# Layer 1's normed rows turned by VectorE and through DRAM instead of by TensorE

## The chip, the cores and the metric

The kernel runs on one core of one Trainium2 chip. A core has a matrix engine (TensorE, PE in the profile; its weight loads are PEld), a vector engine (VectorE, DVE), a scalar engine (ScalarE, ACT), a general engine (GpSimd, POOL) and SyncE (SP), which here issues transfers. Sixteen DMA engines move data between DRAM and the on-chip SBUF. TensorE writes to PSUM, a small accumulator memory of banks. The metric is the device time of one launch in microseconds, smaller is better.

## The reference, cut to what matters

Two layers, each attention and then a feed-forward part, each part followed by a residual and a layer norm over rows of 512 numbers, on 8 batches of 512 tokens:

```
x = layernorm(x + attention0(x))           # 16 heads of 32, causal
x = layernorm(x + top-2 of 8 experts(x))   # with low-rank additions
x = layernorm(x + attention1(x))           # below
x = layernorm(x + quantised_ffn(x))        # integer weights, 1408 hidden

def attention1(x):                         # 8 query heads of 64, 2 key/value groups
    nrm = norm(x, over the row) * 512 ** -0.5
    h = norm_scale * x / (nrm + 1e-8) * split_scale
    q, k, v = h @ Wq.T, h @ Wk.T, h @ Wv.T
    attn = softmax(q k^T / 8)              # no mask
    return (attn v) @ Wo.T
```

The experts' result is normed, and those rows are normed again into h. The change is in how h reaches the form that q, k and v need it in: columns of 512 on partitions, tokens along the free dimension (hT). Because attention 1 has no mask, the order of the 512 tokens inside a batch does not matter to softmax as long as keys and values agree and the query rows are put back.

## The kernel before, in words

All arithmetic is float32; a float32 matmul shows as two instructions, so x8 in a timeline is four matmuls. The program runs attention 0 (up to about 760 us), then the experts over gathered tiles of 128 tokens (to about 1190 us), attention 1 (to about 1766 us) and the quantised feed-forward part.

*The expert tiles.* `Tiles.step` handles one tile of 128 tokens in about 5.8 us: gate and up products (`gate_up`), ScalarE's Silu and VectorE's product, two transposes with a ScalarE copy (`turn_hidden`), down products (`down`), an output copy by VectorE or ScalarE in turn, and a store of the tile's results by SP (L871; the y buffer has two copies). TensorE's order is as written; the other engines are placed by a scheduler. In `usual_pass`, a table called `beside` puts other pieces between tiles, among them `Attention1.first_pieces`: the preparation of batch 0 for attention 1, one piece every second tile.

*Preparing a batch for attention 1* (`Attention1.prepare`). `fetch` gathers the two experts' result rows of 128 tokens (indirect transfers issued by POOL into the buffers rows0 and rows1); `add` sums them into x with their weights and takes row statistics (VectorE); `deviations` takes roots (POOL); `norm` writes the normed rows xn over the buffer rows0 (VectorE, four 128x512 instructions, L714). `turn(c)`, for c = 0 to 3, transposes four 128x128 blocks of xn into one PSUM bank by TensorE (L1477), and ScalarE copies the bank into hT and multiplies by the per-column scale nss, the product of the two norm scales (L1478). `key` (L1484), `value` (L1493) and `query(g)` (L1503) multiply hT by the weights held in `attn1_qkv` and ScalarE copies the results out. hT has one buffer: the next batch's hT can be written once this batch's query(3) has read it.

*The attention loop* (`batches`). Each batch has 8 steps. A step issues two pairs of score matmuls (L1584), whose exponentials ScalarE takes (L1587); then VectorE adds the exponentials of the step before (`add`, L1595); then come the pieces that `plan` lists for this step; then the products with v of the step before (L1606). After every second step `normalise` multiplies the sums by a block of ones (row sums, L1614), ScalarE copies them (L931), VectorE takes a reciprocal (L1617) and multiplies the product by it into `aoT` (L1618), and POOL keeps a running total of the reciprocals (L934). Here TensorE, VectorE, ScalarE and POOL all run strictly in the order written; SP's order is left to the scheduler. PSUM for single products (`mm`) has two banks.

Within batch b's steps, `plan` places the remaining queries of b, the output projection of batch b - 1 for four groups of rows (`project`: matmuls L1552, then VectorE's residual L1558 and statistics L1566), and the preparation of batch b + 1: fetch at step 0, adds, deviations at 4, norm at the front of step 5, the four turns and key at 6, value and query(0) at 7. It also places conversions of the integer weights of the last part (`weights.convert`, VectorE L994 and L926), each followed by the next load into the same single buffer (`weights.load`, L980, issued by SP): that load waits until the conversion has read the buffer. Batch 0 has its own places, and so has the last batch.

Of the kernel before, what the change touches and what calls it, by code (L numbers as in the profile page):

```python
# [9 lines left out]
F32 = mybir.dt.float32  # L10
# [3 lines left out]
AF = mybir.ActivationFunctionType  # L14
ALU = mybir.AluOpType
# [3 lines left out]
P = 128  # L19
NB = 8  # L20
S = 512
D = 512
NT = S // P
ND = D // P
# [39 lines left out]
class Inputs:  # L64
# [3 lines left out]
    def __init__(self, *aps):  # L68
        for name, ap in zip(self.names, aps, strict=True):
            setattr(self, name, ap)  # L70


class Env:
# [928 lines left out]
class IntegerFfn:  # L1002
# [64 lines left out]
    def out(self, os, t, c, parts):  # L1067
        for i, h in enumerate(parts):
            self.nc.tensor.matmul(os[t], lhsT=h[:, ts(t, P)], rhs=self.weights(2 * NHID + c),  # L1069
                                  start=(c, i) == (0, 0), stop=(c, i) == (NHID - 1, 1))  # L1070
# [374 lines left out]
class Attention1:  # L1445
# [2 lines left out]

    HD = 64

    def __init__(self, env, guard, router, rows, own, p_mm):
        self.env, self.nc, self.guard, self.router, self.own, self.p_mm = env, env.nc, guard, router, own, p_mm
        self.rows = rows

        self.w_qkv = own.tile([P, UPS, 512], F32, name="attn1_qkv")
        env.load_units(self.w_qkv, 0, env.ins.w_attn1[:6])
        self.nss = env.norm_scales()
        self.state = {}
# [4 lines left out]
    def prepare(self, b):  # L1463


        nc, own, w_qkv = self.nc, self.own, self.w_qkv
        st = self.state[b] = {"qT": [None] * ND}
        combine = Combine(self.router, b, self.rows, ("rows0", "rows1"))

        def norm():  # L1470
            st["xn"], st["scale"] = combine.norm()
            st["hT"] = own.tile([P, ND, S], F32, tag="hT", name="hT1")

        def turn(c):
            ps = self.mm([P, S], "ps_hT")
            for t in range(NT):
                nc.tensor.transpose(ps[:, ts(t, P)], st["xn"][:, t, ts(c, P)], self.env.ident)  # L1477
            nc.scalar.activation(st["hT"][:, c, :], ps, AF.Copy, scale=self.nss[:, c : c + 1])  # L1478

        def key():  # L1480
            hT = st["hT"]
            ps = self.mm([P, S], "ps_k1")
            for c in range(ND):
                nc.tensor.matmul(ps, lhsT=w_qkv[:, 4, ts(c, P)], rhs=hT[:, c, :], start=c == 0, stop=c == ND - 1)  # L1484
            st["kT"] = own.tile([P, S], F32, tag="kT", name="kT", bufs=2)
            nc.scalar.copy(st["kT"], ps)

        def value():
            hT = st["hT"]
            ps = self.mm([P, NT, P], "ps_v1")  # L1490
            for t in range(NT):
                for c in range(ND):
                    nc.tensor.matmul(ps[:, t, :], lhsT=hT[:, c, ts(t, P)], rhs=w_qkv[:, 5, ts(c, P)],  # L1493
                                     start=c == 0, stop=c == ND - 1)
            st["v"] = own.tile([P, NT, P], F32, tag="v", name="v1", bufs=2)
            nc.scalar.copy(st["v"], ps)

        def query(g):

            hT = st["hT"]  # L1500
            ps = self.mm([P, S], "ps_q1")
            for c in range(ND):
                nc.tensor.matmul(ps, lhsT=w_qkv[:, c, ts(g, P)], rhs=hT[:, c, :], start=c == 0, stop=c == ND - 1)  # L1503
            st["qT"][g] = (self.work if g % 2 else own).tile([P, S], F32, tag="qT", name="qT")
            nc.scalar.copy(st["qT"][g], ps)  # L1505

        return {"fetch": combine.fetch, "add": combine.add, "sum": combine.sum, "stat": combine.stat, "deviations": combine.deviations, "norm": norm,
                "turn": turn, "key": key, "value": value, "query": query}

    def first_pieces(self):  # L1510

        do = self.first = self.prepare(0)
        return ([lambda t=t: do["fetch"](t) for t in range(NT)] + [lambda t=t: do["add"](t) for t in range(NT)]
                + [do["deviations"], do["norm"]] + [lambda c=c: do["turn"](c) for c in range(ND)]
                + [do["key"], do["value"], lambda: do["query"](0)])

    def run(self, weights, split):

# [7 lines left out]
    def batches(self, work, p_sc, p_av, weights, split):  # L1526
        env, nc, guard, state, HD = self.env, self.nc, self.guard, self.state, self.HD
        xs = env.xs
        scale = 1.0 / math.sqrt(HD)
# [81 lines left out]
        def normalise(b, g, total, av):  # L1611
            rs = self.mm([P, S], "rs1")
            for j in range(2):
                nc.tensor.matmul(rs[HD * j : HD * (j + 1), :], lhsT=ones, rhs=total[:, j, :], start=True, stop=True)  # L1614
            r_inv = work.tile([P, S], F32, tag="r_inv", name="r_inv1")
            guard.watch_sums(rs, r_inv)
            nc.vector.reciprocal(r_inv, r_inv)  # L1617
            nc.vector.tensor_tensor(state[b]["aoT"][:, g, :], av, r_inv, ALU.mult)  # L1618
            guard.watch_inverses(r_inv)

        def plan(b):


            todo = [[] for _ in range(ND * NT // 2)]
            here = pieces.pop(b)
            first, final = b == 0, b == NB - 1
            then = None if final else self.prepare(b + 1)
            if not final:
                pieces[b + 1] = then
                todo[0] += [lambda t=t: then["fetch"](t) for t in range(NT)]  # L1630
            for g, i in zip((1, 2, 3), (1, 3, 5) if first else (0, 1, 5) if final else (0, 1, 3)):
                todo[i].append(lambda g=g: here["query"](g))
            if b:
                for t, i in enumerate((2, 3, 4, 7) if final else (2, 3, 4, 5)):
                    todo[i].append(lambda t=t: project(b - 1, t))
                if not final:
                    todo[6].append(lambda: norm(b - 1))
            if final:
                for c, i in enumerate((0, 2, 4, 6)):
                    todo[i].append(lambda c=c: split(0, c, self.mm([P, S], "ps_xT")))  # L1640
            else:
                if first:

                    for t, i in ((2, 1), (3, 2)):
                        todo[i].append(lambda t=t: then["sum"](t))
                        todo[i + 2].append(lambda t=t: then["stat"](t))
                for t, i in ((0, 1), (1, 2)) if first else ((0, 2), (1, 2), (2, 3), (3, 4)):
                    todo[i].append(lambda t=t: then["add"](t))
                todo[4].append(then["deviations"])

                todo[5].insert(0, then["norm"])
                todo[6] += [lambda c=c: then["turn"](c) for c in range(ND)]
                todo[6].append(then["key"])
                todo[7] += [then["value"], lambda: then["query"](0)]
            for i in (7,) if first else (1, 7):
                todo[i] += [weights.convert, lambda: weights.load(work, 2, weights.FIRST)]
            return todo

# [34 lines left out]
def usual_pass(tc, ins, held_out):  # L1693
    nc = tc.nc
    with ExitStack() as ctx:
# [4 lines left out]
        with tc.tile_pool(name="a_mm", bufs=2, space=PSUM) as p_mm, ExitStack() as attn1_ctx:  # L1700
            with tc.tile_pool(name="routes", bufs=1, side="right") as routes, \
                    tc.tile_pool(name="experts", bufs=1, side="right") as pool, ExitStack() as tiles_ctx:
                experts = Experts(env, pool)
                router, tiles, tables = attention0(env, guard, keep, routes, experts, dram, p_mm, tiles_ctx)

                def load_rows(b):
                    rows = router.rows[S * b : S * (b + 1)]
                    nc.sync.dma_start(out=env.xs[b], in_=rows.rearrange("(t p) d -> p t d", p=P))

                env.open_stream(ctx, range(NB // 2))  # L1710
                rows = ctx.enter_context(tc.tile_pool(name="c_rows", bufs=1))
                own = attn1_ctx.enter_context(tc.tile_pool(name="c_own", bufs=1))
                attention = Attention1(env, guard, router, rows, own, p_mm)
                beside = {tiles.next + 6 * (b + 1): lambda b=b: load_rows(b) for b in range(NB // 2)}

                for i, piece in enumerate(attention.first_pieces()):
                    beside[E * NT + 4 + 2 * i] = piece
                with in_order(tc):
                    while tiles.next < tiles.n:
                        tiles.step()  # L1720
                        next(tables, None)
                        beside.pop(tiles.next, lambda: None)()
                assert not beside and next(tables, None) is None
                tiles.rare()
# [314 lines left out]
```

## Time and profile before

| what | us |
|---|---|
| median of three runs | 2284.05 |
| the runs | 2281.4 to 2284.93 |
| the profiled execution | 2286.21 |
| its span, first to last instruction | 2284.5 |
| TensorE busy (98% of the span) | 2238.4 |
| VectorE busy (54%) | 1242.0 |
| ScalarE busy (28%) | 648.2 |
| POOL busy (22%) | 496.2 |
| TensorE, transposes of xn into ps_hT, 128 | 20.2 |
| ScalarE, scaled copies into hT, 32 | 20.5 |
| VectorE, normed rows xn, 32 | 15.4 |

Busy times are sums over instructions; matmuls are pipelined, so a group's busy time is not the same as the time it holds TensorE. In a timeline each line has a start in us from the first instruction, a duration in us, the engine, the line of the kernel, the operation, written tile and read tiles, the shape and the count; what stands in brackets is how long the engine was idle before, and what it waited for. In a list of waits the numbers are us in total, times, and the longest. In a table of stretches the columns are the stretch, its length, busy time and count of PE, PEld, DVE, ACT and POOL, the granted clock of TensorE, the busy share of the DMA engines and GB/s.

### The profile page before, as it was taken

How to read it: one execution, taken by the hardware profiler on the slowest of the kernel's cores; microseconds unless marked ns; L12 is line 12 of the kernel's file. 1: busy time of each engine (PE TensorE's matmuls, PEld its weight loads, DVE VectorE, ACT ScalarE, POOL GpSimd, SP SyncE). 2: the span in 40 equal slices, each digit the busy share in tenths (PEclk: the TensorE clock that was granted, in tenths of full speed). 3: DMA queues.
4: the chain of work that ended last, by engine and by line, in shares of the span. 5: the costliest groups of instructions: out<-in, count | busy, mean ns of one | idle time of the engine just before them, and what ended most of it. 6: DMA issues, size and time to landing. Idle time of an engine off the chain costs nothing. (4 is left out here: it accounts for less than half of the span.)

```text
span 2284.5 us, 24183 instructions
## 1 busy us (share of the span) xinstructions
PE 2238.4 (98%) x9430; PEld 1153.0 (50%) x9430; DVE 1242.0 (54%) x1976; ACT 648.2 (28%) x937; POOL 496.2 (22%) x489
## 2 busy tenths in 40 slices
PE   9999999999998999999999999999999999999997
PEld 3344444444443444444443334443343777887776
DVE  3457576566657433242216877787667544444443
ACT  2332322323323221111223323333332222222222
POOL 2232423313233241131115122322211000000000
PEclk9999999999999999999999999999999999999999
DMA  8010101101112224232224011100100100000000
GB/s 290 19 56 1 56 19 37 56 1 56 47 45 74 93 85 174 91 125 88 92 84 147 10 56 56 49 27 27 37 1 17 48 19 19 19 19 19 19 19 20
DMA packets 58444, 126.63 MB, mean 55 GB/s; under 512 B 6210, under 2 KB 6210, under 8 KB 58322
## 3 DMA queue, kind: packets, MB, share of 16 engines
q1 hardware_dynamic: 47040, 89.32, 11.1%
q0 software_dynamic: 10560, 34.61, 5.2%
q8 instruction: 77, 1.26, 0.2%
q10 hardware_dynamic: 722, 1.07, 0.1%
q14 instruction: 45, 0.37, 0.0%
HBM read 89.59 MB, written 35.39 MB: 55 GB/s over the span
## 5 line engine op out<-in xcount | busy, mean ns | idle before, releaser
L845 PE MATMUL ps_gu<-experts,xrT 128*128 128x512 f32 (+1 forms) x520 | 248.7, 601 | 0.0
L1268 ACT ACTIVATE p<-sc 128x2048 f32<-128x2048 f32 (+1 forms) x96 | 152.9, 1593 | 189.0 <-PE sc L1264 189.0
L1273 POOL TENSOR_SCALAR_AFFINE_SELECT p<-p 128x512 f32<-128x512 f32 x128 | 93.2, 743 | 380.1 <-ACT p L1268 374.0
L1060 DVE SCALAR_TENSOR_TENSOR hT<-ps_u,vec,sg 128x512 f32<-128x512 f32 x88 | 65.8, 748 | 198.4 <-PE ps_u L1055 198.4
L1069 PE MATMUL ps_f<-ffn_w,h_half 128*128 128x512 f32 x672 | 169.8, 393 | 1.6 <-DVE h_half L1064 1.1
L934 POOL TENSOR_TENSOR g_total<-g_total,r_inv 128x512 f32<-128x512 f32 x64 | 89.7, 1402 | 359.7 <-DVE r_inv L1617 283.3
L1617 DVE RECIPROCAL r_inv<-r_inv 128x512 f32<-128x512 f32 x32 | 106.9, 3339 | 97.5 <-ACT r_inv L931 97.5
L1587 ACT ACTIVATE p<-sc 128x1024 f32<-128x1024 f32 x128 | 124.0, 1021 | 125.9 <-PE sc L1584 125.9
L1296 DVE TENSOR_TENSOR p<-p 128x1536 f32<-128x1536 f32 (+2 forms) x96 | 129.2, 1345 | 38.7 <-POOL p L1273 21.7
L1069 PEld LDWEIGHTS ps_f<-ffn_w,h_half 128*128 128x128 f32 x672 | 124.3, 188 | 34.9 <-DVE h_half L1064 7.6
L1055 PE MATMUL ps_g<-x_high,ffn_w 128*128 128x512 f32 x352 | 141.0, 401 | 0.8 <-DVE x L1558 0.8
L848 DVE TENSOR_TENSOR h<-ps_gu,h 128x256 f32<-128x256 f32 x67 | 28.4, 423 | 205.6 <-ACT h L847 205.6
L1055 PE MATMUL ps_g<-x_low,ffn_w 128*128 128x512 f32 x352 | 139.0, 395 | 0.0
L1055 PE MATMUL ps_u<-x_low,ffn_w 128*128 128x512 f32 x352 | 138.8, 394 | 0.0
L1055 PE MATMUL ps_u<-x_high,ffn_w 128*128 128x512 f32 x352 | 138.6, 394 | 0.0
L862 PE MATMUL ps_y<-experts,hT 128*128 128x512 f32 (+1 forms) x272 | 127.9, 593 | 0.5 <-ACT hT L856 0.5
L1584 PE MATMUL sc<-qT,kT 64*128 64x512 f32 x512 | 127.2, 615 | 1.0 <-ACT qT L1505 0.7
L1200 PE MATMUL ps_q<-experts 128*128 128x512 f32 x256 | 121.2, 615 | 4.3 <-DMA experts<-in_xT 4.3
L845 PEld LDWEIGHTS ps_gu<-experts,xrT 128*128 128x128 f32 x520 | 89.6, 192 | 68.2 <-issue 68.1
L1606 PE MATMUL av<-p,v 128*64 128x512 f32 x512 | 123.7, 605 | 0.0
L1193 PE MATMUL ps_v<-experts 128*128 128x512 f32 x256 | 116.3, 602 | 2.1 <-DVE v L1195 2.1
L1552 PE MATMUL ps_o<-attn_out,aoT 128*128 128x512 f32 x256 | 117.3, 602 | 0.8 <-ACT r_inv L931 0.8
(256 smaller groups left out, 3532.3 us busy)
## 6 DMA issues: line engine op xcount, KB each, us to landing
results<-y SPq DMA_DIRECT2D x68, 256.0 KB, 2.0
x<-in_x SPq DMA_DIRECT2D x8, 1024.0 KB, 7.5
experts<-in_gate_up SPq DMA_DIRECT2D x8, 1024.0 KB, 11.7
rows<-x SPq DMA_DIRECT2D x32, 256.0 KB, 2.1
x<-rows SPq DMA_DIRECT2D x8, 1024.0 KB, 11.3
experts<-in_xT SPq DMA_DIRECT2D x7, 1024.0 KB, 5.5
out<-x SPq DMA_DIRECT2D x28, 256.0 KB, 2.3
ffn_i<-in_wq_ffn SPq DMA_DIRECT2D x11, 512.0 KB, 4.3
```

What stands on the lines that cost most here:

```text
L845: mm = nc.tensor.matmul(ps, lhsT=xT[:, c, :], rhs=self.weights(i, c), start=c == 0, stop=c == ND - 1)
L862: self.nc.tensor.matmul(ps, lhsT=hT[:, c, :], rhs=self.weights(i, ND + c), start=c == 0, stop=c == self.NI - 1)
L1055: nc.tensor.matmul(ps, lhsT=w[:, ts(dc, P)], rhs=x[:, dc, :], start=(dc, i) == (0, 0), stop=(dc, i) == (ND - 1, 1))
L1069: self.nc.tensor.matmul(os[t], lhsT=h[:, ts(t, P)], rhs=self.weights(2 * NHID + c), start=(c, i) == (0, 0), stop=(c, i) == (NHID - 1, 1))
L1193: nc.tensor.matmul(ps, lhsT=xts[b][:, c, ts(t, P)], rhs=wv[:, c, :], start=c == 0, stop=c == ND - 1)
L1200: nc.tensor.matmul(ps, lhsT=wq[:, g, ts(c, P)], rhs=xts[b][:, c, :], start=c == 0, stop=c == ND - 1)
L1268: nc.scalar.activation(p, sc[:, :, :width], AF.Exp, scale=scale)
L1296: nc.vector.tensor_tensor(total[:, :, P * kt :], total[:, :, P * kt :], p[:, :, at : at + w], ALU.add)
L1552: nc.tensor.matmul(ps, lhsT=state[b]["aoT"][:, c, ts(t, P)], rhs=w_out[:, c, :], start=c == 0, stop=c == ND - 1)
L1584: nc.tensor.matmul(sc[:, j, :], lhsT=st["kT"][hs, ts(kt, P)], rhs=st["qT"][g][hs, :], start=True, stop=True)
L1587: nc.scalar.activation(p, sc, AF.Exp, scale=scale)
L1606: nc.tensor.matmul(st["av"][HD * j : HD * (j + 1), :], lhsT=st["v"][:, kt, HD * j : HD * (j + 1)], rhs=p[:, j, :], start=kt == 0, stop=kt ...
```

## The change

1. **The transposes.** `turn` is gone. A new class `Turn` holds a DRAM buffer. `blocks(t)` lets VectorE transpose each 32x32 block of one group of 128 normed rows, into a room of 128x2048 (the buffer rows1). After the fourth group, `out` stores the room in four transfers, one for each block of 32 partitions, so that in DRAM row p holds column p of each chunk; `back` loads 128 rows of 8 KB into hT. In the turned hT the tokens of a batch stand in another order: blocks of 32 from the four groups by turns.
2. **The order of tokens.** Queries, keys and values take that order from hT. In `normalise` the product with the reciprocal reads both operands in runs of 32 and writes `aoT` in the natural order.
3. **The scales.** nss is multiplied into the weights once, by ScalarE, in eight instructions beside the expert tiles (`scale`, with batch 0's fetches).
4. **The places.** For batches 2 to 7: adds at steps 1, 1, 2, 3 (before: 2, 2, 3, 4), deviations at 3, norm and the blocks at the front of step 4, key at 6. For batch 1, prepared in batch 0's loop: norm and blocks at 5, key at 7, and query(3) of batch 0 at step 4 instead of 5. One conversion moves from step 1 to step 0.

In the built program SP's queue holds, in batch 0's loop, the four stores of `out`, then one integer-weight load, then `back`; in the later loops `back` stands directly behind the four stores.

```
+class Turn:
+    N = P // 32
+    def __init__(self, env, dram, n, name):
+        self.nc, self.n = env.nc, n
+        self.dram = dram.tile([P, ND, self.N, n * 32], F32, name=name)
+    def blocks(self, room, t, x):
+        out = room.rearrange("p (j t c) -> p j t c", t=self.n, c=32)[:, :, t, :]
+        self.nc.vector.transpose(out, x.rearrange("p (j c) -> p j c", c=32))
+    def out(self, room):
+        for i in range(self.N):
+            src = room[32 * i : 32 * (i + 1), :].rearrange("r (k j f) -> r k j f", j=self.N, f=self.n * 32)
+            self.nc.sync.dma_start(out=self.dram.rearrange("(j r) k i f -> r k j i f", j=self.N)[:, :, :, i, :], in_=src)
+    def back(self, room):
+        self.nc.sync.dma_start(out=room, in_=self.dram.rearrange("p k i f -> p (k i f)"))
+    def by_tile(self, a, turned):
+        if turned:
+            return a.rearrange("p (i t c) -> p t i c", i=self.N, c=32)
+        return a.rearrange("p (t i c) -> p t i c", i=self.N, c=32)
...
         def norm():
             st["xn"], st["scale"] = combine.norm()
-            st["hT"] = own.tile([P, ND, S], F32, tag="hT", name="hT1")
-        def turn(c):
-            ps = self.mm([P, S], "ps_hT")
-            for t in range(NT):
-                nc.tensor.transpose(ps[:, ts(t, P)], st["xn"][:, t, ts(c, P)], self.env.ident)
-            nc.scalar.activation(st["hT"][:, c, :], ps, AF.Copy, scale=self.nss[:, c : c + 1])
+        def blocks(t):
+            if t == 0:
+                st["room"] = self.rows.tile([P, ND * S], F32, tag="rows1", name="turned")
+            self.turn.blocks(st["room"], t, st["xn"][:, t, :])
+            if t == NT - 1:
+                self.turn.out(st["room"])
+                st["hT"] = own.tile([P, ND, S], F32, tag="hT", name="hT1")
+                self.turn.back(st["hT"].rearrange("p k s -> p (k s)"))
...
+    def scale(self, c):
+        for part in (self.w_qkv[:, c, :], self.w_qkv[:, ND : ND + 2, ts(c, P)]):
+            self.nc.scalar.mul(part, part, self.nss[:, c : c + 1])
...
-            nc.vector.tensor_tensor(state[b]["aoT"][:, g, :], av, r_inv, ALU.mult)
+            nc.vector.tensor_tensor(self.turn.by_tile(state[b]["aoT"][:, g, :], False), self.turn.by_tile(av, True),
+                                    self.turn.by_tile(r_inv, True), ALU.mult)
...
-            for g, i in zip((1, 2, 3), (1, 3, 5) if first else (0, 1, 5) if final else (0, 1, 3)):
+            for g, i in zip((1, 2, 3), (1, 3, 4) if first else (0, 1, 5) if final else (0, 1, 3)):
...
-                for t, i in ((0, 1), (1, 2)) if first else ((0, 2), (1, 2), (2, 3), (3, 4)):
+                for t, i in ((0, 1), (1, 2)) if first else ((0, 1), (1, 1), (2, 2), (3, 3)):
                     todo[i].append(lambda t=t: then["add"](t))
-                todo[4].append(then["deviations"])
-                todo[5].insert(0, then["norm"])
-                todo[6] += [lambda c=c: then["turn"](c) for c in range(ND)]
-                todo[6].append(then["key"])
+                todo[4 if first else 3].append(then["deviations"])
+                i = 5 if first else 4
+                todo[i][:0] = [then["norm"]] + [lambda t=t: then["blocks"](t) for t in range(NT)]
+                todo[7 if first else 6].append(then["key"])
                 todo[7] += [then["value"], lambda: then["query"](0)]
-            for i in (7,) if first else (1, 7):
+            for i in (7,) if first else (0, 7):
                 todo[i] += [weights.convert, lambda: weights.load(work, 2, weights.FIRST)]
```

## The prediction, made before the changed kernel was run

> **What bounds the kernel now.** I read the busy shares first. TensorE is the bound nearly everywhere; VectorE has room on the average only.
>
> ```profile
> PE 2238.4 (98%) x9430; PEld 1153.0 (50%) x9430; DVE 1242.0 (54%) x1976; ACT 648.2 (28%) x937; POOL 496.2 (22%) x489
> ```
>
> Second, TensorE's timeline through step 6 of one layer-1 batch (start, duration, line, tile, count, idle before): the stage that the change cuts.
>
> ```profile
> 1518.35 1.99 PE L1584 MATMUL sc<-qT,kT 64*128 64x512 f32 x8
> 1520.27 1.40 PE L1477 MATMUL ps_hT<-ident,xn 128*128 128x128 f32 x8
> 1522.14 1.24 PE L1477 MATMUL ps_hT<-ident,xn 128*128 128x128 f32 x8 [0.47 <-ACT hT L1478]
> 1523.58 3.70 PE L1484 MATMUL ps_k<-hT,attn_qkv 128*128 128x512 f32 x8 [0.20 <-ACT hT L1478]
> ```
>
> The transposes with their two waits hold TensorE from 1520.27 to 1523.58: 3.31 us, in each of seven batches.
>
> Third, VectorE's timeline of that batch, since it will now make the turned rows.
>
> ```profile
> 1477.02 3.35 DVE L1617 RECIPROCAL r_inv<-r_inv 128x512 f32<-128x512 f32 x1 [9.15 <-ACT r_inv L931]
> ...
> 1505.17 2.52 DVE L1595 TENSOR_TENSOR total<-total,p 128x1024 f32<-128x1024 f32 x2
> ...
> 1515.71 0.69 DVE L1618 TENSOR_TENSOR aoT<-av,r_inv 128x512 f32<-128x512 f32 x1
> 1516.32 1.72 DVE L1595 TENSOR_TENSOR total<-p,p 128x1024 f32<-128x1024 f32 x1
> ...
> 1518.39 1.92 DVE L714 TENSOR_SCALAR xn<-x,mv,dev 128x512 f32<-128x512 f32 x4
> ```
>
> The reader is to see that VectorE idles 9.15 us before 1477.02 and is then busy almost without a gap until the normed rows at 1518.39: locally, the chain to hT is VectorE's, not TensorE's.
>
> Fourth, DMA issues (KB each, median us to landing), and what SP's weight loads wait for.
>
> ```profile
> rows<-x SPq DMA_DIRECT2D x32, 256.0 KB, 2.1
> x<-rows SPq DMA_DIRECT2D x8, 1024.0 KB, 11.3
> experts<-in_xT SPq DMA_DIRECT2D x7, 1024.0 KB, 5.5
> ffn_i<-in_wq_ffn SPq DMA_DIRECT2D x11, 512.0 KB, 4.3
> ```
>
> ```profile
> SPq L980 <- DVE ffn_w L994: 294.2, 12, 50.2
> ```
>
> SP does wait for VectorE's conversions before those loads, 294.2 us in 12 waits; whatever stands behind one waits too.
>
> Fifth, three stretches around TensorE's longest hole (2.89 us, until 736.58).
>
> ```profile
> 733.00:737.00 4.00, 1.11 (x4) 0.30 (x4) 4.00 (x12) 0.60 (x1) 1.32 (x1) 1.00 0.00 0
> 737.00:744.00 7.00, 6.27 (x16) 1.42 (x13) 2.18 (x11) 2.37 (x5) 4.60 (x4) 0.51 0.00 0
> ```
>
> The granted clock (third number from the right) is 0.51 for 7 us after it; after the 1.78 us hole at 984 it stays 1.00.
>
> **The change, part by part.** The sum is made against the profiled execution, 2286.21 us (span 2284.5), 2.2 above the median of the runs, 2284.05.
>
> *Removed.* 128 transposes and 32 scaled copies (ScalarE, 0.69 each). In the seven batches this is up to 3.31 us each. For batch 0, beside the expert tiles, four groups of four, 0.53 us each (start of such a group to the next instruction): -2.1.
>
> *Scales into the weights.* Eight ScalarE products, 128x512 near the 0.69 of a 128x512 row, half-size ones near 0.37. The built order puts the first right after the output copy of 853.80, four tiles before its place in the code, while attn_qkv lands only at 858.22; behind it on ScalarE stands the hidden rows' copy of 856.74, which TensorE needs at 857.91. So about 859.4, a wait of 1.5 us. Bounds 0 (landing three microseconds earlier) and 5. I take +1.5. On SP, batch 0's four outs and the back stand among the tiles' result stores; those behind the back wait up to 6.1 us for the outs, but a tile takes 5.8 and its y buffer is written again two tiles later, so 11.6 less the 2.0 of a store covers it: 0. Tile phase together: -0.6.
>
> *Ordinary batches (preparing batches 2 to 7).* VectorE's new order, by the rows above: reciprocal at 1477.02, product, sum (5.7); two rows' adds moved up from step 2 (2.37 each, start to start); sums 2.5; residual 0 1.6; add 2.4; reciprocal, product, sum 5.7; residual 1 waits for its matmuls, 1501.0; add; sums, ending at 1507.5; normed rows at 1509.8. The conversion moved to step 0 falls in the 9.15 us hole and costs nothing; if that hole were gone, its 1.9 us would delay hT directly. Deviations keep their place in POOL's order; the gathers, issued from 1462.6 to 1473.7 and 3.9 us each, land before the first moved add at 1482.7.
>
> Four 32x32 transposes of 128x512: unseen. Bounds 0.48 (xn, start to start) and 3.4 (reciprocal); I take 0.62, near the other one-pass rows of this shape (product 0.61, statistics 0.73): end at 1512.2. The product read in runs of 32 keeps 0.69; bounds 0.69 and twice that, two of them in the chain.
>
> Out: four issues of 0.32 to 0.43 us on SP, 256 KB each, as 512-byte pieces: 128 per DMA engine. The trace's single packets took 9 ns at 32 B, 84 at 2048, 159 at 4096, so about 28 at 512: 3.6 us, up to 1.6 times that since each issue reads only 32 partitions (the 16-partition lora loads' 7168-byte packets took a median 659 ns against 271 by that line). With 0.85 to the first packet and 0.4 to land, 4.8 to 7; I take 6.1. Bounds: 3.0 (2.0 of results<-y plus three issues) and 11.3. Back: 1 MB in rows of 8 KB: in_xT's 5.5 was shared with x's load; I take 4.6, bounds 3.6 (fastest ffn_i) and 11.3. With 0.15 for SP's wake-ups 10.85: hT lands at about 1523.1. The key matmuls want it at 1520.27 (no transposes before them now) and began at 1523.58: -0.4 a batch, six times -2.6. TensorE waits about 2.9 us where it transposed for 3.3; behind that wait stands every later matmul, and SP's next loads, harmlessly, behind its own. Break-even is a round trip of 11.2.
>
> The Trainium skill, DMA: Bandwidth & Descriptors, Anatomy of one DMA, fits 2.0 us plus bytes over 436 GB/s, for SWDGE. By it both ways take an estimated 8.8 us, the six batches give -14 and the whole sum is about 11 lower. The 5.5 us row for 1 MB stands above the fit's 4.4, so I stay with the row.
>
> A hole of 2.9 us can halve the clock, as before 737; at 1.78 it doesn't. I take a quarter of six batches at 2.6 us (half clock for 3.4 to 7 us): +4, bounds 0 and 20. The Trainium skill, TensorE: Matmul & The Clock Gate, Part 1, gives a free-running window of 3413 ns that must be idle: by it a 2.9 us hole alone cannot fill the window and the +4 would be an estimated 0. Here the clock fell after 2.89 us.
>
> *Batch 0's loop (preparing batch 1).* Here I expect the loss. Query 3 moves before step 4's sums, so its reciprocal moves from 1220.36 to 1223.3; then product, sum, normed rows (before: 1226.50), transposes, ending at 1233.8. Only then come step 5's sums (1236.4), for which TensorE's row sums wait: reached at 1230 (its matmuls added up without transposes and key), so a hole of 6.5 us. Then scores, to 1240, and key now waits for hT. But SP's built order has the next integer-weight load between the four outs and the back; it waits for step 7's conversion on VectorE, behind another reciprocal, product and sum: about 1245.9. The back follows it in the rings: 5.7 us from there, 1251.7. Key 3.63, halved clock 2.6: values start at 1258 instead of 1239.54: +18. Bounds: +10 if the load costs the back nothing and the clock holds; +24 if back is as slow as x<-rows.
>
> **Sum:** -0.6 - 2.6 + 4 + 18 = +18.8: 2305.0 beside the profiled 2286.2, 2303 on the median.
>
> **Rivals.** (1) Faster: the round trip is hidden in the six batches. Place: the hT wait before key; price -3.3 a batch, -19.9 in all, no clock loss: -0.6 - 19.9 + 18 = -2.5, 2281.5. It decides below a round trip of about 8.3 us after the last transpose. For it: idle DMA engines there. Against: the issue-to-landing rows alone give 2.0 + 1.0 + 5.5. (2) The way through DRAM is slow, 14 us by small pieces and half the partitions: +2.8 a batch and a halved clock of 2.6 each time: +32, with the rest +49.8, 2334. For it: lora's slow packets; against: the linear packet times. (3) VectorE becomes the bound: a transpose as slow as the reciprocal, 2.7 us more, 11 a batch: 66 + 11 in batch 0, + 18 and clock: about 2390. Nothing speaks for it but that the row is missing.
>
> **How the numbers follow.** Forecast 0.62, (1) 0.13, (2) 0.20, (3) 0.05. Something within 0.2% (4.6 us, what a measurement of this kernel can tell from no change) lies between forecast and (1). The forecast's own range is 2290 to 2318: batch 0 from +10 to +24 and the batches a microsecond each way. The 8-in-10 range takes half of (2) and stops short of (1) and (3): 2287 to 2332. Faster 0.10, same 0.06, slower 0.84.
>
> **What would show it.** Right: no ps_hT matmuls on xn; key behind a DMA wait of 2 to 4 us in six batches, and of ten or more in batch 0, preceded by a hole before rs; out about 6, back about 4.6 us to landing; clock under 1.00 after batch 0's hole. Wrong: key starting straight after scores, the back issued before the load, or transposes far from 0.62 us.

## The result, and the profile after

The changed kernel takes 2321.92 us (median of four runs, 2321.36 to 2328.4) against 2282.77 us before (2281.4 to 2284.93): 1.0177 times the time, 95% interval 1.0157 to 1.0198. The profiled executions are 2322.22 and 2286.21 us, their spans 2320.4 and 2284.5: 35.9 us more. The medians are 39.2 us apart, about twice the 18.8 of the forecast, which named 2303; the time lies inside the stated range (2287 to 2332) and outside the forecast's own (2290 to 2318).

Where the 35.9 us lie follows from TensorE's timeline alone, by marks that both kernels have: attention 1's first score matmul, and the first value matmul of each batch from 1 to 7.

| stretch | before | after | forecast | measured |
|---|---|---|---|---|
| start to first score | 1191.92 | 1190.34 | -0.6 | -1.6 |
| first score to batch 1's values | 47.62 | 66.47 | +18 | +18.9 |
| batch 1's values to batch 7's, six batches | 438.47 | 457.20 | -2.6 + 4 | +18.7 |
| batch 7's values to the last matmul | 594.98 | 594.90 | 0 | -0.1 |

In the changed kernel TensorE is busy for 96% of a longer span, where it was 98%.

```profile
PE 2231.7 (96%) x9302; PEld 1144.4 (49%) x9302; DVE 1265.3 (55%) x2008; ACT 632.4 (27%) x913; POOL 505.6 (22%) x489
```

TensorE's waits of the changed kernel (line, what released it, us in total, times, longest) name three new ones. Before, key waited 1.4 us in all for ScalarE's copies of hT, the projections 0.8 us in all, and the row sums not at all.

```profile
PE ps_k L1519 <- DMA hT<-turned: 32.7, 7, 12.7
PE ps_o L1601 <- DVE x L1607: 8.9, 6, 1.5
PE rs L1663 <- DVE total L1644: 6.2, 1, 6.2
```

The first and third belong in part to batch 0's loop. TensorE's timeline there, after the change:

```profile
1234.59 1.98 PE L1663 MATMUL rs<-total,ones 128*64 128x512 f32 x4 [6.20 <-DVE total L1644]
1236.50 2.59 PE L1633 MATMUL sc<-qT,kT 64*128 64x512 f32 x8
1251.76 5.21 PE L1519 MATMUL ps_k<-hT,attn_qkv 128*128 128x512 f32 x8 [12.67 <-DMA hT<-turned]
```

And SP's timeline of the same stretch (start and duration of the issue):

```profile
1232.13 3.25 SPq L93 DMA_DIRECT2D turned<-turned  x4
1243.81 0.38 SPq L1012 DMA_DIRECT2D ffn_i<-in_wq_ffn  x1
1244.37 0.34 SPq L96 DMA_DIRECT2D hT<-turned  x1
```

The four stores of out are issued from 1232.13 and have landed at 1238.57. Then SP stands still until the conversion has freed the integer buffer, issues that load at 1243.81, and only then the back, at 1244.37.

The six ordinary batches, one of them on TensorE after the change; its counterpart of before is the fence in the prediction that shows L1477.

```profile
1537.75 1.99 PE L1633 MATMUL sc<-qT,kT 64*128 64x512 f32 x8
1541.22 3.70 PE L1601 MATMUL ps_o<-attn_out,aoT 128*128 128x512 f32 x8 [1.48 <-DVE x L1607]
1544.86 1.94 PE L1655 MATMUL av<-p,v 128*64 128x512 f32 x8
1546.72 1.99 PE L1633 MATMUL sc<-qT,kT 64*128 64x512 f32 x8
1551.89 5.33 PE L1519 MATMUL ps_k<-hT,attn_qkv 128*128 128x512 f32 x8 [3.18 <-DMA hT<-turned]
```

There are two holes, of 1.48 and 3.18 us, and the key matmuls themselves take 5.33 where they took 3.70. VectorE and POOL in the same batch:

```profile
1531.70 2.52 DVE L1644 TENSOR_TENSOR total<-total,p 128x1024 f32<-128x1024 f32 x2
1535.79 0.16 DVE L742 SCALAR_TENSOR_TENSOR dev<-dev 128x4 f32<-128x4 f32 x1 [1.57 <-POOL dev L735]
...
1536.23 1.92 DVE L746 TENSOR_SCALAR xn<-x,mv,dev 128x512 f32<-128x512 f32 x4
1538.06 2.48 DVE L88 STREAM_TRANSPOSE turned<-xn 128x512 f32<-128x512 f32 x4
1540.47 0.70 DVE L1607 SCALAR_TENSOR_TENSOR x<-x,dev,ps_o 128x512 f32<-128x512 f32 x1
```

```profile
1531.88 1.10 POOL L733 TENSOR_SCALAR dev<-mv 128x4 f32<-128x4 f32 x1 [6.21 <-DVE mv L727]
1532.96 0.21 POOL L734 TENSOR_SCALAR dev<-mv 128x4 f32<-128x4 f32 x1
1533.25 2.50 POOL L735 TENSOR_TENSOR dev<-dev,pos_half 128x8 f32<-128x8 f32 x1
```

The reader is to see that VectorE has ended the sums at 1534.2 and waits 1.57 us for POOL's deviations, whose input, the statistics of the fourth add, came only at 1531.8. Behind that wait stand the normed rows, the transposes, and the residual L1607, for which TensorE's next projection waits 1.48 us: the bank of `mm` that it is to write (the row sums have the other in between) is freed by that residual.

The transfers of the changed kernel (KB each, median us to landing):

```profile
turned<-turned SPq DMA_DIRECT2D x32, 256.0 KB, 3.9
hT<-turned SPq DMA_DIRECT2D x8, 1024.0 KB, 4.9
```

In the batch above the transposes end at 1540.47, the first store is issued at 1540.57, the last lands at 1546.96, the back is issued at 1547.02 and lands at 1551.84. The round trip is 11.4 us: 6.5 out, 4.9 back.

The granted clock of TensorE (third number from the right; 1.00 is full speed) in the stretches behind two of the waits for hT, and across a third:

```profile
1323.00:1330.00 7.00, 6.77 (x16) 2.71 (x18) 1.92 (x4) 0.59 (x1) 0.82 (x1) 0.76 0.00 0
1399.50:1406.00 6.50, 6.29 (x20) 2.21 (x20) 1.92 (x4) 0.59 (x1) 0.74 (x1) 1.00 0.01 3
1702.50:1711.00 8.50, 8.27 (x16) 3.16 (x18) 2.11 (x5) 0.59 (x1) 1.09 (x1) 0.63 0.00 0
```

Those holes were 3.41, 3.48 and 3.17 us long. The clock fell after the first and the third and not after the second, which was the longest of the three.

The six batches add up: transposes and their waits gone, 6 x -3.31 = -19.9; waits for hT, +20.0; waits for the residual, 6 x 1.48 = +8.9; together 9.0 of the 18.7. Slow clock adds 8.9 to key and what follows it (1.6, 0, 2.7, 1.6, 0 and 3.0, read as the time from key's first matmul to the 34th after it, less the 9.05 us that it takes undisturbed). The last 0.8 is not placed.

### The profile page after: what moved, and what is told of

Same layout as the page of the kernel before. It is cut to its first block, busy times and chain, and to the rows that moved or that the text cites. A ratio compares the mean times of both kernels' runs of the same rounds, so it can differ in the third digit from the quotient of the medians.

```text
span 2320.4 us, 24012 instructions
## 1 busy us (share of the span) xinstructions
PE 2231.7 (96%) x9302; PEld 1144.4 (49%) x9302; DVE 1265.3 (55%) x2008; ACT 632.4 (27%) x913; POOL 505.6 (22%) x489
```

## The experiments

The first score lay between 1188.6 and 1194.7 us in the profiled executions of these kernels, although the changed one and the next seven do not differ before it, so single profiles are compared from the first score on. The columns are the first two stretches of the table above, per batch for the six, and the timed comparison with the kernel before, which ran beside each group (medians 2283.9 and 2284.9 beside the runs of this section). Kernels are told apart by their edit to the changed kernel.

| kernel | first score to batch 1's values | mean period of the six | median us | ratio to before |
|---|---|---|---|---|
| before | 47.62 | 73.08 | 2282.8 | 1 |
| changed | 66.47 | 76.20 | 2321.9 | 1.0177 (1.0157 to 1.0198) |
| SP as written | 58.83 | 76.50 | 2319.5 | 1.0143 (1.0126 to 1.0161) |
| query 3 at step 5 | 65.27 | 76.47 | 2323.3 | 1.0169 (1.0152 to 1.0186) |
| both of these | 56.42 | 76.37 | 2314.2 | 1.0129 (1.0114 to 1.0145) |
| residual first | 67.60 | 78.61 | 2339.7 | 1.0241 (1.0224 to 1.0258) |
| key at 7 | 67.64 | 72.65 | 2302.7 | 1.0084 (1.0067 to 1.0101) |
| early adds | 67.22 | 71.87 | 2300.7 | 1.0066 (1.0047 to 1.0085) |
| early adds, key at 7 | 67.00 | 69.68 | 2285.1 | 0.9998 (0.9988 to 1.0007) |
| the same, batch 1 by TensorE | 47.37 | 69.65 | 2266.5 | 0.9921 (0.9908 to 0.9935) |

### Batch 0's loop: the load ahead of the back

```
-            with in_order(self.env.tc, mybir.EngineType.DVE, mybir.EngineType.Activation, mybir.EngineType.Pool):
+            with in_order(self.env.tc, mybir.EngineType.DVE, mybir.EngineType.Activation, mybir.EngineType.Pool,
+                          mybir.EngineType.SP):
```

> Attention 1's transfers on SP go out in the order of the code, so that in batch 0's loop the back stands ahead of the integer-weight load. Theory A (the load between the outs and the back is what makes batch 1's keys late): the outs land at 1238.6 as in the changed kernel, the back is issued at once and takes the 4.9 us of the other batches, hT at 1243.5 instead of 1251.7; the hole before key shrinks from 12.7 to about 4.5 us; the six later batches stay as they are; 2322 - 8 = 2314. Theory B (the way through DRAM is itself slow there, the rings being busy): the back lands at most 2.5 us sooner, 2319. Theory C (the load has nothing to do with it): key at 1251.8, 2322.

SP's and TensorE's timelines of this kernel (it starts attention 1 at 1194.67, 4.3 us later than the changed one):

```profile
1236.18 3.25 SPq L93 DMA_DIRECT2D turned<-turned  x4
1242.77 0.35 SPq L96 DMA_DIRECT2D hT<-turned  x1
1247.86 5.81 SPq L1012 DMA_DIRECT2D ffn_i<-in_wq_ffn  x2
```

```profile
1238.65 1.98 PE L1664 MATMUL rs<-total,ones 128*64 128x512 f32 x4 [6.19 <-DVE total L1645]
1240.55 2.69 PE L1634 MATMUL sc<-qT,kT 64*128 64x512 f32 x8
1247.74 5.92 PE L1519 MATMUL ps_k<-hT,attn_qkv 128*128 128x512 f32 x8 [4.49 <-DMA hT<-turned]
```

The back goes out behind the stores and takes about 4.9 us; the hole before key is 4.49 us instead of 12.67, as theory A had it, and from first score to values it is 7.6 us less. Theories B and C fall: 7.6 us of the loss of batch 0's loop is the order of SP's queue. The hole of 6.2 before the row sums is untouched. The time fell by less than that, 2.4 us on the medians; in the profiled execution the first score came 4.3 us later and the six batches took 1.8 us more. Where the same edit is made on top of the next one, the medians show it in full, 2323.3 to 2314.2.

### Batch 0's loop: query 3

```
-            for g, i in zip((1, 2, 3), (1, 3, 4) if first else (0, 1, 5) if final else (0, 1, 3)):
+            for g, i in zip((1, 2, 3), (1, 3, 5) if first else (0, 1, 5) if final else (0, 1, 3)):
```

> Query 3 of batch 0 goes back to step 5; all else as changed. Theory A (its place delays VectorE's reciprocal, and with it norm, transposes and sums): reciprocal at 1218.8 instead of 1221.7, transposes end at about 1229.2, sums at 1231.7, TensorE reaches the row sums at about 1228.2, so the hole before them shrinks from 6.2 to 3.5 us; the load behind the conversion still stands ahead of the back, the conversion comes about 3 us sooner, so key at about 1248.9; 2322 - 3 = 2319. Theory B (the transposes ahead of the sums make the hole whatever query 3 does): hole 6 us as before, key unmoved, 2322.

```profile
1233.25 1.97 PE L1663 MATMUL rs<-total,ones 128*64 128x512 f32 x4 [3.41 <-DVE total L1644]
1250.85 6.63 PE L1519 MATMUL ps_k<-hT,attn_qkv 128*128 128x512 f32 x8 [13.16 <-DMA hT<-turned]
```

The hole before the row sums is 3.41 us (3.5 expected by theory A), so query 3's place is worth 2.8 us of the 6.2; the rest is the normed rows and transposes that stand ahead of the sums. Key starts 58.8 us after the first score instead of 61.4, as expected too. But the values gain only 1.2 us: key ran slower after a hole of 13.2 us, 6.63 against 5.21 us. The time is the same as the changed kernel's (2323.3), where 2319 was expected.

> Transfers on SP in the order of the code, and query 3 of batch 0 back at step 5. Theory A (the load ahead of the back and query 3's place are two separate costs of batch 0's loop): transposes end 38.7 us after the first score of attention 1, outs 6.5 us later, the back 5 us after that, so key 50.2 us after the first score instead of 61.4 in the changed kernel and 58.8 with query 3 moved alone; from the first score to batch 1's values 56.7 instead of 66.5; what is left of the loss there against the 47.6 of the kernel before, 9 us, is the round trip itself and the transposes ahead of the sums; 2322 - 10 = 2312. Theory B (the two overlap, one hides the other): no better than the better one, 58.8, 2314.

With both edits the values come 56.42 us after the first score (56.7 expected), and 2314.2 us is measured where 2312 was expected. At key's start the two add: 8.4 us sooner by SP's order alone, 2.6 by query 3 alone, 10.9 by both. What is left, 8.8 us over before, is in this timeline: 3.41 us of sums behind the transposes, a wait of 4.57 us for the round trip, and a slow clock, less the transposes that TensorE no longer does.

```profile
1230.62 1.72 PE L1664 MATMUL rs<-total,ones 128*64 128x512 f32 x4 [3.41 <-DVE total L1645]
1232.26 3.00 PE L1634 MATMUL sc<-qT,kT 64*128 64x512 f32 x8
1239.82 6.04 PE L1519 MATMUL ps_k<-hT,attn_qkv 128*128 128x512 f32 x8 [4.57 <-DMA hT<-turned]
```

### Six batches: is the wait for the residual a cost of its own?

```
                 i = 5 if first else 4
-                todo[i][:0] = [then["norm"]] + [lambda t=t: then["blocks"](t) for t in range(NT)]
+                at = 0 if first else len(todo[i])
+                todo[i][at:at] = [then["norm"]] + [lambda t=t: then["blocks"](t) for t in range(NT)]
```

> In the loops of batches 1 to 6, step 4's projection with its residual and statistics goes ahead of the normed rows and the transposes on VectorE. Theory A (VectorE's chain to hT decides, and TensorE's 1.48 us wait for the residual only takes time off the later wait for hT): the residual fills the 1.57 us in which VectorE waits for POOL's deviations, transposes end at the same place, the 1.48 us wait is gone, the wait for hT grows from 3.3 to 4.8 us, the period stays at 76.2 us on the mean apart from the clock, which the longer hole can only lower more often; 2322 to 2331. Theory B (the residual wait is a cost of its own): 6 x 1.48 = 8.9 us less, 2313.

```profile
1549.84 3.70 PE L1601 MATMUL ps_o<-attn_out,aoT 128*128 128x512 f32 x8
1553.47 1.94 PE L1655 MATMUL av<-p,v 128*64 128x512 f32 x8
1555.34 1.99 PE L1633 MATMUL sc<-qT,kT 64*128 64x512 f32 x8
1562.95 6.62 PE L1519 MATMUL ps_k<-hT,attn_qkv 128*128 128x512 f32 x8 [5.63 <-DMA hT<-turned]
```

The wait of 1.48 us is gone (no bracket on ps_o), nothing is gained in the period (78.61 us, 2.4 more), and the wait for hT grows to between 5.6 and 6.7 us. Theory B falls: taking this wait off TensorE's path, ahead of a later one, gave nothing. The size was missed, 2339.7 where 2322 to 2331 was expected. Two reasons show in the profile: the residual, put first, waits 0.92 us for its own matmuls, so the transposes end 0.9 us later than if it had only filled VectorE's idle time; and the clock now falls after every one of the six holes, 2.8 to 3.0 us each, against 1.5 on the mean in the changed kernel.

### Six batches: key a step later

```
-                todo[7 if first else 6].append(then["key"])
+                todo[7].append(then["key"])
```

> In the loops of batches 1 to 6, key goes from step 6 to the front of step 7; all else as changed. Theory A (the round trip is 11.3 us long and only key's place makes TensorE wait for it): TensorE reaches key 4.7 us later, at 1553.3 in the batch where hT lands at 1551.8, so no wait; the 20.0 us of waits for hT in six batches and the 9.2 us of halved clock behind them go; the 1.48 us wait for the residual stays; period 73.07 - 3.31 + 1.48 = 71.2 us; 2322 - 29 = 2293. Theory B (with key out of the way another wait takes its place, the row sums on VectorE being late): the period stays above 74, 2310 or more.

```profile
1532.04 3.70 PE L1601 MATMUL ps_o<-attn_out,aoT 128*128 128x512 f32 x8 [1.49 <-DVE x L1607]
1535.67 1.94 PE L1655 MATMUL av<-p,v 128*64 128x512 f32 x8
1537.54 1.99 PE L1633 MATMUL sc<-qT,kT 64*128 64x512 f32 x8
1539.45 1.94 PE L1655 MATMUL av<-p,v 128*64 128x512 f32 x8
1542.70 1.08 PE L1663 MATMUL rs<-total,ones 128*64 128x512 f32 x4 [1.31 <-DVE total L1644]
```

The waits for hT and all losses of clock behind them are gone, as theory A had it. But the period is 72.65 us in all six batches, not 71.2: TensorE now reaches step 6's row sums before VectorE has the sums, and waits 1.31 us. Neither theory was whole: the round trip is hidden by a later key, and VectorE's late chain then takes back 1.49 + 1.31 of the 3.31 us.

### Six batches: the adds a step earlier

```
-                for t, i in ((0, 1), (1, 2)) if first else ((0, 1), (1, 1), (2, 2), (3, 3)):
+                for t, i in ((0, 1), (1, 2)) if first else ((0, 1), (1, 1), (2, 2), (3, 2)):
                     todo[i].append(lambda t=t: then["add"](t))
-                todo[4 if first else 3].append(then["deviations"])
+                todo[4 if first else 2].append(then["deviations"])
```

> In the loops of batches 1 to 6 the fourth add goes from step 3 to step 2 and the deviations with it; key stays at step 6. Theory A (the late end of VectorE's chain to the transposes, the 1.57 us wait for POOL's deviations with it, is what takes the gain): transposes end about 2.5 us sooner, the residual is no longer late, so no 1.48 us wait; the wait for hT goes from 3.3 to about 2.3; period 76.2 - 2.5 = 73.7 us if the clock falls as often, 72.2 if holes of 2.3 us leave it alone: 2322 - 15 = 2307 down to 2298. Theory B (VectorE is full, and work moved ahead delays its reciprocals and sums by as much): row sums wait, period 76 as before, 2322.

VectorE around the transposes, POOL's deviations, and TensorE's key in this kernel:

```profile
1518.81 2.52 DVE L1644 TENSOR_TENSOR total<-total,p 128x1024 f32<-128x1024 f32 x2
1521.25 0.16 DVE L742 SCALAR_TENSOR_TENSOR dev<-dev 128x4 f32<-128x4 f32 x1
```

```profile
1511.71 0.23 POOL L733 TENSOR_SCALAR dev<-mv 128x4 f32<-128x4 f32 x1 [14.71 <-DVE mv L727]
1511.91 0.22 POOL L734 TENSOR_SCALAR dev<-mv 128x4 f32<-128x4 f32 x1
1512.21 1.67 POOL L735 TENSOR_TENSOR dev<-dev,pos_half 128x8 f32<-128x8 f32 x1
```

```profile
1465.50 3.70 PE L1519 MATMUL ps_k<-hT,attn_qkv 128*128 128x512 f32 x8 [1.72 <-DMA hT<-turned]
```

The deviations are ready 7 us before VectorE asks for them, VectorE does not wait, the residual wait is gone, and hT is waited for by 1.66 to 1.93 us. The period is 71.5 us in five batches and 73.5 in one, whose key ran at a lowered clock after a hole of 1.93 us. That is below both values expected (73.7 and 72.2). Theory A holds, with a larger gain than its sum: 2300.7 us, 21 less than the changed kernel, by moving one add and three POOL instructions one step. The transposes end 52.15 us after the batch's first value matmul, where it was 54.87. Of these 2.7 us 1.57 is VectorE's wait for POOL; 0.98 is a wait for a projection's matmuls that VectorE had ahead of the residual at 1527.72 in the changed kernel, and that the moved add fills. No run has the one without the other.

This edit together with key at step 7:

> The fourth add and the deviations at step 2, and key at step 7, in the loops of batches 1 to 6. Theory A (with key at 7 alone the period is 72.65 us because VectorE's wait for POOL makes the residual late by 1.48 us and the row sums of step 6 by 1.31): without that wait both are gone, the period is 73.07 - 3.31 = 69.8 us, six times 2.9 less than with key at 7 alone: 2303 - 17 = 2286, that is about the kernel before, batch 0's loop still losing 19. Theory B (VectorE has become the bound of a batch whatever the order): the period stays at 72.0 or more, 2299 or more.

TensorE in one of its batches, at the places of the three waits:

```profile
1518.46 3.70 PE L1601 MATMUL ps_o<-attn_out,aoT 128*128 128x512 f32 x8
1527.94 1.08 PE L1663 MATMUL rs<-total,ones 128*64 128x512 f32 x4
1530.87 3.70 PE L1519 MATMUL ps_k<-hT,attn_qkv 128*128 128x512 f32 x8
```

With key at step 7 as well, no TensorE wait for hT or for the residual remains in the six batches, and the period is 69.68 us, 3.4 less than before, where 69.8 was expected. In the batch shown the row sums start 0.3 us late, in the other five they do not wait. VectorE is not the bound of a batch in this order. At 2285.1 us, the time is that of the kernel before: what the six batches gain, batch 0's loop loses.

### A version below both kernels

```
+        def turn(c):
+            if c == 0:
+                st["hT"] = own.tile([P, ND, S], F32, tag="hT", name="hT1")
+            ps = self.mm([P, S], "ps_hT")
+            for t in range(NT):
+                nc.tensor.transpose(ps[:, ts(t, P)], st["xn"][:, t, ts(c, P)], self.env.ident)
+            nc.scalar.copy(st["hT"][:, c, :], ps)
...
+                if first:
+                    todo[5].insert(0, then["norm"])
+                    todo[6] += [lambda c=c: then["turn"](c) for c in range(ND)]
+                else:
+                    at = 0
+                    todo[i][at:at] = [then["norm"]] + [lambda t=t: then["blocks"](t) for t in range(NT)]
+                todo[6 if first else 7].append(then["key"])
```

with query 3 of batch 0 at step 5, the early adds, `normalise`'s product without runs of 32 for batch 1, and `scale(t)` called with the adds of batch 0.

> As the run with early adds and key at 7, and besides batch 1 is turned by TensorE as in the kernel before (with plain copies, its tokens in natural order, query 3 of batch 0 at step 5, key at 6), and the scales are multiplied into the weights with the adds of batch 0 instead of its fetches. Theory A (what the changed kernel loses is batch 0's loop, 18.9 us, VectorE's late chain in the others, and 2.1 us of TensorE's wait for the scaled weights): from the first score to batch 1's values 47.6 us as before, six periods of 69.8, no hole at the scaling, and the 1.7 us of batch 0's transposes saved: 2284 - 20 - 2 = 2262. Theory B (VectorE bounds a batch at 72.0 or more): 2276 or more.

It takes 2266.5 us, 0.9921 of before (0.9908 to 0.9935), 18 us less. Batch 0's loop is back at 47.37 us and the six periods at 69.65 on the mean, both as theory A had them. The expected 2262 was missed by 4.5. One part did nothing: with `scale(t)` called 46 us later in the code the built ScalarE order still has the products in the same place, and TensorE still waits 1.4 us there. The rest is not placed; it is no larger than the variation ahead of the first score (1192.9 here). Of the waits that the change brought two are left on TensorE's list: that one (`ps_y`), and 1.1 us more than before at `ps_hT`, the expert tiles' transposes, behind VectorE.

```profile
PE ps_hT L886 <- DVE h L880: 2.9, 3, 1.4
PE ps_y L894 <- issue: 1.4, 1, 1.4
```

## Why the prediction was right or wrong

**Direction, and batch 0's loop: right, and by its own steps.** The first score came 1.58 us earlier than in the frame of the prediction; with that added, what was foreseen and what was measured are: end of the transposes 1233.8 and 1233.6; hole before the row sums 6.5 and 6.2; the load's issue 1245.9 and 1245.4; hT 1251.7 and 1253.3; start of the values 1258 and 1258.4. Two terms missed, with opposite signs: hT came 7.9 us behind the load's issue where 5.7 was taken, and from key to the values it was 5.05 us where 3.63 + 2.6 was taken. So the last agreement is in part luck. Of the 18.9 us SP's order carries 7.6, shown by putting the back ahead; query 3's place moves key by 2.6, shown by moving it back; 8.8 are left with both.

**The six batches: wrong, +18.7 for +1.4.** The prediction's step that failed is the first of these three terms, in order of size; in the other two the mechanism was right and the size was off.

1. "Deviations keep their place in POOL's order", priced at nothing. The place was kept; the input was not. The adds moved, the fourth one's statistics came only 2.4 us ahead of VectorE's need for the deviations, and POOL's three instructions take 2.2 us at best (1511.71 to 1513.88 in the run with early adds) and 3.9 beside VectorE's sums (1531.88 to 1535.75). VectorE's sums ended where they were foreseen: 50.5 us after the scores of step 7 (1483.68 in the batch shown), where the working had 1507.5 - 1456.86 = 50.6. Then came 1.57 us that the working did not have. It should have asked of the moved norm what it reads and who writes that, POOL included. TensorE saw 1.48 of it at the projection, 6 x 1.48 = 8.9 us. Moving the fourth add and the deviations took this wait away and gave back 21 on the medians: it also filled VectorE's other wait of 0.98 us, and shortened the holes that lower the clock.
2. The clock: +4 taken, with bounds 0 and 20; 8.9 measured, 4.9 more. The mechanism was right and the size was off: a quarter of six batches at 2.6 us was taken, and four of six batches lost 1.6 to 3.0 us.
3. The round trip: 10.85 taken, 11.4 measured. The stores took 6.5 instead of 6.1, the back 4.9 instead of 4.6. The wait for hT became 3.3 us on the mean instead of 2.9, 2.7 us in six batches. The four transposes (0.62 taken, 0.60 from start to start) and the product in runs of 32 (0.69 taken and measured) were right.

The three make 8.9 + 4.9 + 2.7 = 16.5 of the 17.3 us between +18.7 and +1.4; 0.8 is not placed.

That the residual would make TensorE wait was not foreseen either: nothing was said of what stands behind the normed rows on VectorE. The run with the residual first shows that it was no cost of its own, since the wait for hT followed.

**Rivals.** Rival 2 gave 2334 and lies nearer to the measured 2321.9 than the forecast's 2303 does, but its mechanism is not what happened: it needed a round trip of 14 us and 2.6 us of slow clock in every batch, and this one has 11.4 and 1.5 on the mean. The range held because it reached towards that rival, and not for a reason named in it: that is luck. Rival 1 needed 8.3 us (8.1 by the working's own times, 1520.27 - 1512.2). Rival 3 had the transposes at 3.4 us; they took 0.66. What rival 3 described did happen in a small way, VectorE's chain deciding the batch, but by an order and a wait, not by the length of an instruction: with early adds and key at 7 the same instructions fit in 69.68 us.

**Tile phase.** -0.6 was foreseen; -1.6 was measured to the first score, but 3.8 us of that were won before 806 us, ahead of anything that the change touches. From there on it is +2.2: a wait of 2.10 us for the hidden rows behind the scaled weights (1.5 taken), -1.7 for the 16 transposes (2.1 taken), +0.7 where VectorE's transposes stand ahead of an expert tile's product (nothing was taken), +2.0 for a hole of 2.10 us at 984.56, which was 1.77 before, and the slow matmuls behind it, and -0.8 for a wait for a row copy that fell away.

## What to carry to other kernels

When a piece of work is moved forward on one engine, list everything that it reads and what writes that, small instructions on side engines too: here three POOL instructions on 4 and 8 numbers per partition took 3.9 us, more than the four large transposes (2.5), and held them up by 1.57. Work that is moved from the bounding engine to a longer way round pays as far as that way is hidden, by a later consumer or an earlier start: the period was 73.08 us before and 76.20 as changed, 72.65 with key one step later, 71.87 with the adds one step earlier, and 69.68 with both. And look in the built order of a transfer queue for strangers between two dependent transfers: one load between the stores and the back cost 7.6 us.

## What was not expected of the hardware

*The clock after a hole.* Behind TensorE's waits for hT the loss was read as above, up to the 34th matmul after key's first. After holes of 1.3 to 1.5 us (key at 7, twelve holes, at the projection and the row sums) there was none: the granted clock was 1.00 from 1260 to 1690 us, and the six periods are equal. After 1.66 to 1.93 (early adds, six) there was one loss, of 1.7. After 3.1 to 3.5 us (four kernels, 24 holes) five had none, eleven 1.4 to 1.7, and eight 2.7 to 3.0. After 5.6 to 6.7 (residual first, six) all had 2.8 to 3.0. So between these groups the chance rises with the length, the loss comes in two sizes, and the length alone does not decide: of the 24 holes, the seven of 3.41 us and more brought a loss four times, the seventeen shorter ones fifteen times. The stretch behind the hole of 1.93 us:

```profile
1537.20:1543.00 5.80, 5.73 (x10) 2.23 (x12) 2.00 (x5) 0.30 (x1) 0.98 (x1) 0.71 0.00 0
```

The Trainium skill, TensorE: Matmul & The Clock Gate, section "Why this matters for your kernels", advises against holes above about 3 us, one idle window. The free-running window that Part 1 of that page describes would fit losses that depend on where the hole falls. But here a fall came after 1.93 us of idle time, and five holes above 3.1 us brought none, so the advice is neither a safe side nor a threshold in this kernel.

*POOL beside VectorE's sums.* The three instructions of the deviations took 1.10, 0.21 and 2.50 us while VectorE added two tiles from SBUF (1531.70 to 1534.2), and 0.23, 0.22 and 1.67 us while VectorE took a reciprocal, in the same form and on the same sizes. Over the eight batches the median of the third is 2.50 in the changed kernel and 1.67 with early adds; in the changed kernel's batch 1, with VectorE idle beside it, it is 1.67 too. The Trainium skill, SBUF — State Buffer, section "Who interferes with whom", says that a VectorE instruction with two inputs in SBUF contends with a GpSimd instruction that reads SBUF. The durations agree with that; no run here separates it from other causes.
